# Moving ScalarE's slot for other stages' pieces from the head of a scan round to behind the first decay

## Chip, cores and metric

The kernel runs on one core of a Trainium2 chip. The metric is the device time of one execution in microseconds (us). An execution that the hardware profiler recorded gives the views shown here; times of the kernel before are given as a median of three further runs.

## What is computed

A network of four layers is applied to a tensor x of 4 images, 56 by 56 positions, 96 channels. Layer 0 and layer 1 are vision blocks whose heart is a selective scan over the 3136 positions of an image in four directions, for 192 channels with 16 states each. Layers 2 and 3 are an attention without softmax and a feed-forward network in rounded arithmetic. The part that takes nearly all the time is this recurrence, cut from the reference:

```python
dt = softplus(dt_raw @ dtw + dtb)
d_a = exp(dt[..., None] * a)                 # decay, per channel and state
d_b = dt[..., None] * b_ssm[:, :, None, :]
def step(h, inp):
    da_t, db_t, x_t, c_t = inp
    h = da_t * h + db_t * x_t[..., None]     # 192 x 16 states
    y_t = jnp.einsum('bds,bs->bd', h, c_t)
    return (h, y_t)
```

What stands around it are layer norms, projections, a convolution, SiLU, GELU and ReLU, all of them on the same 4 images.

## The kernel before

**The scan in rounds.** `scans` walks through 2 layers, 4 images, 4 directions and 7 chunks of 448 positions. A chunk has 8 rounds (two halves `e` of the channels, four quarters `q` of the states), so there are 1792 rounds. A round holds three groups `g` of 128 partitions by 448 positions. Round n consists of:

- `products(n)`: VectorE multiplies `du` with `b` for groups 0 and 1 into `h` (line 719). `b` is a row of matmul output on TensorE, made by `begin` a round ahead (`spread_b`, line 616, one PSUM buffer). The third group's product is made on GpSimd in `begin` (line 714).
- `scan(n, g)`, g = 0, 1, 2: VectorE runs the recurrence over the group (line 726) with the decay factors `da[g]` in PSUM.
- `decay(n + 1, g)`: ScalarE writes the next round's factors exp(na * dt) into `da[g]` (line 678). There is one `da` tile per group, so the decay of a group must wait for the scan of the same group in this round, and the next round's scan must wait for it.
- `kept(n)` and `carried(n + 2)`: ScalarE copies three columns that link one chunk to the next (lines 696 and 691); `h` has three buffers.
- `hc`: GpSimd multiplies the scanned states with `c` (line 767); two rounds later `add_up` has TensorE sum them into `y` (lines 794 and 798), and `keep_sums` has ScalarE copy `y` out every fourth round (line 805), between the second and the third decay.

**The chain to the next chunk's dt.** While a chunk is scanned, the next ones are prepared. `prepare` issues DMAs and a GpSimd multiplication (line 521); `prepare_on_scalar` has ScalarE do the copies to `cf` (lines 489, 491, 587) and the softplus (lines 506 and 508) in fixed rounds; `on_tensor` has TensorE do the matmuls of that chain (lines 448, 609, 496). The fetches of `cb`, `dt` and `du` are DMAs issued by SyncE.

**Pieces of other stages.** All other work (load, middle, branch, fuse, attend) is written as generators, cut into pieces at `yield`. A piece is run in one of two slots of a round: "F" pieces end in ScalarE work, "C" pieces are mostly TensorE and VectorE. `scans` yields "F" or "C" where a slot lies, and `overlap` then issues the pieces that are due and for which there is room: `spend` adds a piece's estimated ScalarE and TensorE time to a backlog, `half_round`, called twice a round, drains it by 0.9 and 2.4, and `room` admits a piece if the backlog with it stays within 4.0 and 7.0. A piece holds at most two PSUM banks (`ps`). Large F pieces contain a SiLU or GELU and hence two table loads (lines 903, 1065, 1074, 1102, 1115, with the return load of line 829), or two ReLU groups (lines 1260 to 1262). `keep_busy` puts warming matmuls with zeros (line 785) into TensorE's queue ahead of `begin`'s matmul, as many as the other work of the round leaves room for.

**Order.** The order on TensorE, ScalarE, VectorE and GpSimd is the order in which the Python code issues the instructions; each engine executes its own list in that order, and semaphores hold an instruction until its inputs and its buffer are there. SyncE's DMAs are placed by the framework's scheduler. So where `scans` yields a slot decides where on each engine's list the pieces stand.

Of the kernel before, what the change touches and what calls it, by code (L numbers as in the profile page):

```python
# [167 lines left out]
class Net:  # L168
# [454 lines left out]
    def scans(self):  # L623

        nc, sp = self.nc, self.sp
        chunks = []
        for l in range(2):
            for i in range(NB):
                for n, (orient, rev) in enumerate(ORDER[l]):
                    for step in range(NCS):
                        ch = Step()
                        ch.l, ch.i, ch.orient, ch.rev, ch.step = l, i, orient, rev, step
                        ch.k = 2 * orient + rev if l == 0 else orient + 2 * rev
                        ch.c = NCS - 1 - step if rev else step  # L640
                        ch.n, ch.first = n, n == 0 and step == 0
                        ch.skip = n == 0
                        ch.opening = ch.skip and (l, i) == (0, 0)
                        ch.last = n == 3 and step == NCS - 1
                        ch.cb, ch.dt, ch.du = [], [], []
                        chunks.append(ch)
        rounds = [(ch, e, q) for ch in chunks for e in range(NE) for q in range(NQ)]
        per = NE * NQ


        da = [self.psum.tile([128, 512], F32, name=f"da{g}")[:, : CS + 4] for g in range(NG)]
        for t in da:
            nc.vector.memset(t, 0.0)

        def steps(n):

            return [(ch, n - per * j) for j, ch in enumerate(chunks[max(0, n // per) : n // per + 3], max(0, n // per))]

        def ahead(n):
            for ch, o in steps(n):  # L660
                self.on_tensor(ch, o)

        for n in range(-14, 0):
            for ch, o in steps(n):
                self.prepare(ch, o)
            if n > -8:
                yield "F", n, 0
            for ch, o in steps(n):
                self.prepare_on_scalar(ch, o)
            ahead(n)  # L670
            if n > -8:
                yield "C", n, 0

        def decay(n, g):

            if n < len(rounds):
                ch, e, q = rounds[n]
                nc.scalar.activation(da[g][:, INNER], ch.dt[e][:, g], AF.Exp, scale=ch.par.na[:, e, q, g : g + 1])  # L678

        def column(t, at):  # L680

            return t[:, at : at + 2 * ROW + 1 : ROW]

        def carried(n):

            if n < len(rounds):
                ch, e, q = rounds[n]
                hs[n] = sp.tile([128, WIDE], F32, name="h", bufs=3)
                if not ch.step:
                    return  # L690
                nc.scalar.copy(column(hs[n], ROW if ch.rev else 1), ch.par.carry[:, e, q])  # L691

        def kept(n):
            ch, e, q = rounds[n]
            if ch.step < NCS - 1:
                nc.scalar.copy(ch.par.carry[:, e, q], column(hs[n], 2 if ch.rev else CS + 1))  # L696

        def own(n):
            ch, e, q = rounds[n]
            return NQ * e + q in (OWN_TAIL if ch.l and ch.i else OWN)  # L700

        hs, bs = {}, {}

        def tokens(t):

            return self.groups(t, 2)[:, :, :CS]

        def begin(n):

            if n < len(rounds):  # L710
                ch, e, q = rounds[n]
                bs[n] = self.spread_b(ch, q)
                if not own(n):
                    nc.gpsimd.tensor_tensor(tokens(hs[n])[:, 2], ch.du[e][:, 2], ch.cb[q][:, 1], ALU.mult)  # L714

        def products(n):
            ch, e, q = rounds[n]
            for g in range(3 if own(n) else 2):
                nc.vector.tensor_tensor(tokens(hs[n])[:, g], ch.du[e][:, g], bs[n], ALU.mult)  # L719

        def scan(n, g):
            ch, e, q = rounds[n]
            c = 1 if ch.step else 0
            way = slice(CS + 1 + c, 1, -1) if ch.rev else slice(2 - c, CS + 2)
            h = hs[n][:, g * ROW :]
            nc.vector.tensor_tensor_scan(h[:, way], da[g][:, way], h[:, way], 0.0, ALU.mult, ALU.add)  # L726

        carried(0)
        carried(1)
        begin(0)  # L730
        self.exp_and_ln()
        self.tables = True
        for g in range(NG):
            decay(0, g)
        late = []
        for n, (ch, e, q) in enumerate(rounds):
            r = NQ * e + q
            products(n)
            for c, o in steps(n):
                self.prepare(c, o)  # L740
            self.half_round()
            strided = [1.5 + 1.5 * ch.orient] * (r % NQ == 2)
            strided += [1.5 + 1.5 * c.orient for c, o in steps(n) for _ in self.projected(c, o)]
            self.spend((0.6, 0.7, 1.7, 0, 0, 0, 0.7, 0.6)[r], (1.3, 1.3, 0, 0, 0, 0, 0.4, 0.4)[r] + sum(strided))
            yield "F", n, r
            for c, o in steps(n):
                self.prepare_on_scalar(c, o)
            ended = late.pop(0) if len(late) == 2 else None
            if ended:
                self.keep_busy(ended[2])  # L750
            begin(n + 1)
            if ended:
                self.add_up(*ended)
            ahead(n)
            self.half_round()
            for g in range(NG):
                if g == 2 and ended and ended[2] == NQ - 1:
                    self.spend(0.6, 0)
                    self.keep_sums(*ended[:3])
                scan(n, g)  # L760
                if g == 2:
                    kept(n)
                decay(n + 1, g)
            yield "C", n, r
            carried(n + 2)
            hc = sp.tile([128, NG, CS], F32, name="hc", bufs=3)
            nc.gpsimd.tensor_tensor(  # L767
                hc, tokens(hs[n]), ch.cb[q][:, 0].unsqueeze(1).to_broadcast([128, NG, CS]), ALU.mult,
            )
            late.append((ch, e, q, hc))  # L770
            del hs[n], bs[n]
        for ended in late:
            self.add_up(*ended)
        self.keep_sums(ch, e, q)
        yield "C", len(rounds), 0
# [655 lines left out]
```

## Time and profile before

| | |
|---|---|
| median of three runs | 7943.03 us (7932.21 to 7953.92) |
| the profiled execution | 7941.06 us, span 7939.3 us |
| granted TensorE clock | 0.913 of full speed |
| rounds of the scan | 1792, between about 88 and 7725 us of the span |
| VectorE in that stretch | 7436 us busy of 7637 |
| ScalarE in that stretch | 5942 us busy |
| TensorE, GpSimd in that stretch | 6728 and 7132 us busy |

In the profile, DVE is VectorE, ACT ScalarE, PE TensorE, POOL GpSimd and SP SyncE. A row of the costliest groups gives line, engine, operation, output and inputs, shapes and count, then the busy time and the mean duration in ns, and after the second bar the time that the engine sat idle just before these instructions, with what ended most of that idling. A row of the waits gives who waited for whom, the total in us, the number of waits and the longest. A row of the timeline gives start and duration in us; "x3" stands for three merged neighbours.

### The profile page before, as it was taken

How to read it: one execution, taken by the hardware profiler on the slowest of the kernel's cores; microseconds unless marked ns; L12 is line 12 of the kernel's file. 1: busy time of each engine (PE TensorE's matmuls, PEld its weight loads, DVE VectorE, ACT ScalarE, POOL GpSimd, SP SyncE). 2: the span in 40 equal slices, each digit the busy share in tenths (PEclk: the TensorE clock that was granted, in tenths of full speed). 3: DMA queues.
4: the chain of work that ended last, by engine and by line, in shares of the span. 5: the costliest groups of instructions: out<-in, count | busy, mean ns of one | idle time of the engine just before them, and what ended most of it. 6: DMA issues, size and time to landing. Idle time of an engine off the chain costs nothing.

```text
span 7939.3 us, 113478 instructions
## 1 busy us (share of the span) xinstructions
PE 6970.5 (88%) x33762; PEld 2314.2 (29%) x33762; DVE 7516.4 (95%) x9603; ACT 6104.3 (77%) x12756; POOL 7165.1 (90%) x3989
## 2 busy tenths in 40 slices
PE   7888888889888988899889988998889988899888
PEld 3222223222222223222222222322233222322234
DVE  6999999999999999999999999999999999999983
ACT  6778878777787768887678876787877877778776
POOL 5999999999998999999999999999999999999981
PEclk8989989989999989989889899999999898998988
DMA  5555655567555765566655666555565555655551
GB/s 181 183 188 190 192 194 188 177 192 228 189 188 177 221 204 177 181 190 212 200 180 177 199 208 209 189 164 170 182 208 182 166 173 191 201 175 166 180 171 55
DMA packets 568240, 1467.54 MB, mean 185 GB/s; under 512 B 108034, under 2 KB 337156, under 8 KB 566756
## 3 DMA queue, kind: packets, MB, share of 16 engines
q1 hardware_dynamic: 566848, 1458.49, 57.7%
q8 instruction: 265, 4.34, 0.2%
q14 instruction: 355, 2.91, 0.1%
q10 hardware_dynamic: 772, 1.80, 0.1%
HBM read 1186.49 MB, written 273.47 MB: 184 GB/s over the span
## 4 chain that ended last, share of the span: by engine, by line
DVE 30%; PE 29%; ACT 19%; issue 14%; POOL 4%; DMA 3%; DVEq 0%; SPq 0%; POOLq 0%; ACTq 0%
DVE h L726 22%; DVE h L719 6%; ACT da L678 6%; PE y L798 6%; PE y L785 5%; PE y L794 3%; POOL hc L767 2%; PE b L616 2%; ACT L829 2%; PE ps L946 2%; ACT Y L805 1%; PE pp L496 1%; PE pp L448 1%; PE ps L823 1%; POOL h L714 1%
## 5 line engine op out<-in xcount | busy, mean ns | idle before, releaser
L726 DVE TENSOR_TENSOR_SCAN h<-da,h 128x449 f32<-128x449 f32 (+1 forms) x5376 | 5469.0, 1070 | 92.7 <-ACT da L678 76.1
L767 POOL TENSOR_TENSOR hc<-h,cb 128x1344 f32<-128x1344 f32 x1792 | 4883.8, 2725 | 456.7 <-DVE h L726 355.8
L678 ACT ACTIVATE da<-dt,na 128x448 f32<-128x448 f32 x5376 | 3342.9, 632 | 890.7 <-DVE h L726 875.7
L719 DVE TENSOR_TENSOR h<-du,b 128x448 f32<-128x448 f32 x3584 | 2023.4, 605 | 107.0 <-PE b L616 76.9
L798 PE MATMUL y<-hc,four 128*32 128x448 f32 x14336 | 1894.4, 603 | 12.3 <-POOL hc L767 12.0
L714 POOL TENSOR_TENSOR h<-du,cb 128x448 f32<-128x448 f32 x1792 | 1753.7, 979 | 45.2 <-ACT h L691 26.4
L785 PE MATMUL y<-w,zeros 128*96 128x448 bf16 x5140 | 1421.0, 395 | 0.0
L616 PE MATMUL b<-cf,sel 128*128 128x448 bf16 x1792 | 671.5, 375 | 605.1 <-DVE h L719 596.1
L785 PEld LDWEIGHTS <-zeros 128*96 128x96 bf16 x5140 | 632.5, 134 | 1172.1 <-issue 1011.5
L448 PE MATMUL pp<-U,wd 96*128 96x448 f32 x896 | 663.7, 829 | 10.0 <-DMA U<-u 4.2
L798 PEld LDWEIGHTS y<-hc,four 128*32 128x32 f32 x14336 | 293.8, 112 | 1134.4 <-issue 636.8
L794 PE MATMUL y<-Y,ident 96*96 96x448 f32 x672 | 538.0, 890 | 39.1 <-ACT Y L805 22.3
L496 PE MATMUL pp<-cf,wd 12*96 12x448 f32 (+1 forms) x896 | 464.5, 599 | 92.5 <-ACT dtc L506 51.2
L521 POOL TENSOR_TENSOR duc<-dtc,U 96x896 f32<-96x896 f32 x224 | 482.8, 2155 | 29.7 <-ACT dtc L508 29.7
L696 ACT COPY carry<-h 128x3 f32<-128x3 f32 x1536 | 301.8, 196 | 241.8 <-DVE h L726 232.6
L805 ACT COPY Y<-y 96x448 f32<-96x448 f32 x448 | 341.9, 763 | 28.6 <-PE y L798 27.9
L691 ACT COPY h<-carry 128x3 f32<-128x3 f32 x1536 | 280.9, 183 | 52.7 <-POOL hc L767 48.8
L587 ACT COPY cf<-pp 64x448 f32<-64x448 f32 x448 | 235.6, 526 | 86.8 <-PE pp L609 78.9
L506 ACT ACTIVATE dtc<-pp,wd 96x448 f32<-96x448 f32 x448 | 281.4, 628 | 15.5 <-PE pp L496 11.7
L616 PEld LDWEIGHTS <-sel 128*128 128x128 bf16 x1792 | 178.5, 100 | 373.1 <-issue 302.5
L823 PE MATMUL ps<-w,cen 96*96 96x448 f32 x458 | 232.7, 600 | 34.4 <-DVE w L1240 11.7
L496 PEld LDWEIGHTS pp<-cf,wd 12*96 12x96 f32 (+1 forms) x896 | 111.4, 162 | 452.9 <-ACT dtc L506 167.2
(383 smaller groups left out, 5354.5 us busy)
## 6 DMA issues: line engine op xcount, KB each, us to landing
cb<-cd SPq DMA_DIRECT2D x896, 448.0 KB, 4.9
dt<-dd SPq DMA_DIRECT2D x448, 672.0 KB, 5.6
du<-dd SPq DMA_DIRECT2D x448, 672.0 KB, 5.4
dd<-dtc SPq DMA_DIRECT2D x672, 112.0 KB, 2.0
dd<-duc SPq DMA_DIRECT2D x672, 112.0 KB, 2.0
win<-m SPq DMA_DIRECT2D x252, 112.0 KB, 4.8
U<-u SPq DMA_DIRECT2D x112, 168.0 KB, 4.6
w<-z SPq DMA_DIRECT2D x84, 224.0 KB, 4.2
```

The costliest lines, as they stand in the source:

```text
L448: self.nc.tensor.matmul(ch.ps.rearrange("p (a b) -> p a b", b=HS), ch.par.wx[:, e], self.in_order(self.U[e], ch.orient, ch.c * CS, CS), st ...
L496: self.nc.tensor.matmul(ch.pd, ch.par.wt[rows, C * e : C * e + C], ch.cf[rows], start=True, stop=True)
L521: self.nc.gpsimd.tensor_tensor(in_rows(ch.duc), in_rows(ch.dtc), u[:, :, lo : lo + CS // HS], ALU.mult)
L616: self.nc.tensor.matmul(ps, self.sel[:, q], self.upper(ch.cf), start=True, stop=True)
L678: nc.scalar.activation(da[g][:, INNER], ch.dt[e][:, g], AF.Exp, scale=ch.par.na[:, e, q, g : g + 1])
L714: nc.gpsimd.tensor_tensor(tokens(hs[n])[:, 2], ch.du[e][:, 2], ch.cb[q][:, 1], ALU.mult)
L719: nc.vector.tensor_tensor(tokens(hs[n])[:, g], ch.du[e][:, g], bs[n], ALU.mult)
L726: nc.vector.tensor_tensor_scan(h[:, way], da[g][:, way], h[:, way], 0.0, ALU.mult, ALU.add)
L767: nc.gpsimd.tensor_tensor(hc, tokens(hs[n]), ch.cb[q][:, 0].unsqueeze(1).to_broadcast([128, NG, CS]), ALU.mult,)
L785: self.nc.tensor.matmul(self.y[:C], self.zeros[:, :C], self.some, start=False, stop=False)
L794: nc.tensor.matmul(o, w, self.in_order(a, ch.orient, ch.c * CS, CS), start=True, stop=False)
L798: nc.tensor.matmul(self.y[32 * n : 32 * n + 32], self.four, hc[:, g], start=n == 3, stop=n == 3 or q == NQ - 1,)
```

## The change

Before, a round yields the F slot at its head: ahead of `prepare_on_scalar`, of `begin(n + 1)`, of the scans and of the first decay. After, it yields F inside the loop over the groups, behind `scan(n, 0)` and `decay(n + 1, 0)`, ahead of `scan(n, 1)`. On ScalarE's list the pieces thus move past `prepare_on_scalar` and the first decay; they now stand between the first and the second decay. On TensorE's list F pieces have next to nothing; on GpSimd's, the few multiplications that F pieces hold move past the product of line 714. As F now comes behind the second `half_round`, the backlog has been drained twice and not once when F pieces ask for room; C pieces find the same draining as before. The DMAs that F pieces issue keep their place between those of `prepare` and of `keep_sums` in the written order.

```diff
@@ -742,7 +742,6 @@
             strided = [1.5 + 1.5 * ch.orient] * (r % NQ == 2)
             strided += [1.5 + 1.5 * c.orient for c, o in steps(n) for _ in self.projected(c, o)]
             self.spend((0.6, 0.7, 1.7, 0, 0, 0, 0.7, 0.6)[r], (1.3, 1.3, 0, 0, 0, 0, 0.4, 0.4)[r] + sum(strided))
-            yield "F", n, r
             for c, o in steps(n):
                 self.prepare_on_scalar(c, o)
             ended = late.pop(0) if len(late) == 2 else None
@@ -761,6 +760,8 @@
                 if g == 2:
                     kept(n)
                 decay(n + 1, g)
+                if g == 0:
+                    yield "F", n, r
             yield "C", n, r
             carried(n + 2)
             hc = sp.tile([128, NG, CS], F32, name="hc", bufs=3)
```

Line numbers in this document are those of the kernel before; in the kernel after, lines 746 to 763 have a number lower by one, and those from 764 on a number higher by one.

## The prediction

> **What bounds the kernel now.** I read the page first: busy shares, then the costliest groups.
>
> ```profile
> span 7939.3 us, 113478 instructions
> PE 6970.5 (88%) x33762; PEld 2314.2 (29%) x33762; DVE 7516.4 (95%) x9603; ACT 6104.3 (77%) x12756; POOL 7165.1 (90%) x3989
> ...
> L726 DVE TENSOR_TENSOR_SCAN h<-da,h 128x449 f32<-128x449 f32 (+1 forms) x5376 | 5469.0, 1070 | 92.7 <-ACT da L678 76.1
> ...
> L678 ACT ACTIVATE da<-dt,na 128x448 f32<-128x448 f32 x5376 | 3342.9, 632 | 890.7 <-DVE h L726 875.7
> L719 DVE TENSOR_TENSOR h<-du,b 128x448 f32<-128x448 f32 x3584 | 2023.4, 605 | 107.0 <-PE b L616 76.9
> ```
>
> VectorE is 95% busy, and two lines make it: three scans (L726) and two products (L719) in each of 1792 rounds. Their starts in the timeline put an undisturbed round at about 4.0 us: 1.12 for the products, about 1.0 from scan to scan. What VectorE waits for is the third column: 92.7 us before scans, mostly for the decay factors `da` from ScalarE, and 107.0 before products, mostly for `b` from TensorE. So only about 200 us can be won in the scan part; there is no such ceiling on what can be lost. Next, whom VectorE waits for:
>
> ```profile
> DVE h L719 <- PE b L616: 76.9, 87, 9.6
> DVE h L726 <- ACT da L678: 76.1, 158, 1.9
> ```
>
> The 76.1 us fall on 158 waits. To see which, I took one round with a large foreign piece from the timeline, ScalarE and then VectorE (start, duration, engine):
>
> ```profile
> 3258.70 0.18 ACT L691 COPY h<-carry 128x3 f32<-128x3 f32 x1
> 3258.89 1.28 ACT L1074 ACT_TABLE_LOAD   x1
> 3260.19 1.16 ACT L1074 ACTIVATE w<-ps,b 128x448 f32<-128x448 f32 x2
> 3261.36 1.28 ACT L829 ACT_TABLE_LOAD   x1
> 3262.66 1.20 ACT L678 ACTIVATE da<-dt,na 128x448 f32<-128x448 f32 x2
> ```
>
> ```profile
> 3258.96 3.05 DVE L726 TENSOR_TENSOR_SCAN h<-da,h 128x449 f32<-128x449 f32 x3
> 3261.93 1.12 DVE L719 TENSOR_TENSOR h<-du,b 128x448 f32<-128x448 f32 x2
> 3263.33 2.07 DVE L726 TENSOR_TENSOR_SCAN h<-da,h 128x449 f32<-128x449 f32 x2 [0.28 <-ACT da L678]
> ```
>
> The first scan ends at 3260.03 (start plus 1.07); call it 0. ScalarE is free from -1.15, but the next decay can't start before 0, as it overwrites the `da` that this scan reads. The piece uses that gap: it runs from -1.14 to +2.61, the decay follows, and VectorE, ready at +3.02 (end of the products), waits 0.28 us. The head of the round is where a large piece costs least.
>
> **What the Trainium skill says.** "ScalarE: Activation LUTs", section "What ACT_TABLE_LOAD costs", gives about 1283 ns for a table load and a further drain of about 1380 ns. The trace agrees with the first (1283 ns) and shows no drain: the ACTIVATE starts 1.30 us after the load. I use the trace. "Perfetto Trace Analysis", section "Identifying the Most-Contended Engine", has the engine with the highest occupancy as the one to look at; that is VectorE here, and its waits explain the time. "Advanced Engine Details and Errata", section "Sequencer Loop", has engine instructions wait in a queue for their semaphores; the trace agrees as far as it goes: ScalarE runs its listed order, with every decay behind the piece listed before it.
>
> **The change part by part.** Nothing is computed more or less. In the instruction order of both programs, 837 rounds have foreign ScalarE work ahead of the first decay before (1356 us by the trace's durations); after, 46 with 26 us still do (pieces begun in the other slot), and 847 with 1338 us have it between first and second decay. Large blocks, over 2.7 us, are as many: 209 before, 206 after. So the earlier draining of the backlog hardly changes the packing: 0, at most 10 us either way.
>
> *First decay.* It no longer waits for a piece. Over all rounds with pieces I added up the waits of the first scan on its decay: 67 us, 48 of them behind large blocks and 19 behind small ones whose TensorE input was late. All go: **-67**.
>
> *Second decay.* In the round above the first decay runs from +0.04 to +0.67, the block takes 3.77 (3258.89 to 3262.66) to +4.44, the second decay ends at +5.07, and VectorE sees it at about +5.11. VectorE, no longer held at the first scan, wants the second at +4.02 (products +3.02, one scan step 1.00). It waits 1.09. In general the wait is block minus 2.68 us, so any piece under 2.7 is free; of the 837 rounds some 630 are, covered by a slack of about 2.2 us that decays have in rounds without a piece. The large blocks, from the table-load rows: L903 56 and L1074 28 at 3.77 (84 x 1.09 = 92 us); L1115 28 at 3.51 (28 x 0.83 = 23); L1065 and L1102 56 at 3.24 (56 x 0.56 = 31); and some 40 double ReLU blocks (L1260 to L1262, twice) at 3.58 (40 x 0.90 = 36). Sum 182.
>
> *Third decay.* In some 50 of these rounds the copy L805 (0.5 to 1.0 us) and the carry copy L696 (0.2) stand between second and third decay; the third is then late by another half microsecond: 25. Where VectorE has one more operation in the round (0.6 us, as L888) or came late anyway, the waits shrink; I take off 17. New waits on decays: **+190** (170 to 230).
>
> *The chain to dt (L489, L587, L506, L508).* It stays at the head and is no longer behind a piece. At 2493.87 a piece with table loads (L1102) held L506 until 2497.11; TensorE's L496 sat idle 2.02 us for it, 6.75 us of convolution stood behind that, `b` came late, and VectorE lost 4.54 us, the largest such wait of this kind in that stretch. Products waiting for `b` two rounds after a large block make about 30 us in 27 rounds (all such gaps, tallied from the trace, 90 us in 120 rounds). Part comes back, since the convolution also needs a bank that the piece itself frees, now later: **-20** (0 to -30).
>
> *TensorE behind the pieces.* A piece ends later by about 1.9 us. TensorE's matmuls of the same round that read its result, or reuse its bank, wait with it, and the next `b` is queued behind them. In the written order some 70 rounds have this dependence on a block of 2.5 us or more. The trace of before can't show it, as it has those pieces early; VectorE is itself 1 us late in these rounds, which covers most. Bound: 0 to 70; I take **+10**. The 125 more warming matmuls (L785, 5140 before, 395 ns) are 49 us of a queue with 12% idle: 0; without that cover some tens of us.
>
> *Queues passed.* On SyncE the stores behind a piece (L912, L922, L1111, L1120) wait up to 1.9 us longer for ScalarE and hold the fetches of `cb`, `dt` and `du` behind them; those are issued three rounds, 12 us, ahead and land in 5 to 6: 0, with some us of cover left. On GpSimd only the 27 multiplications of L931 pass the product L714; L1285 and L1213 wait longer for ScalarE, and hold hc (L767): 0, bound 20. ScalarE's wait for a free `h` (L691) has about 2 us in hand.
>
> Sum: -67 + 190 - 20 + 10 = **+113 us** against the profiled execution of 7941.06 (span 7939.3): 8054. The median shown, 7943.03, is 2 us higher, inside its own spread of 7932 to 7954.
>
> **The rivals.**
> *TensorE gets late too* (0.15). For: in-order queue, 88% busy, PSUM banks shared. Against: VectorE's new lateness covers it. 113 + 60 = 173: 8114 and up.
> *The head of the chain is what counts, and it is faster* (0.05). With the chain to dt always first, TensorE is never held and `b` never late: up to 107 us at L719 and the 67 at L726 come back, 174 in all. That decides only if the new waits on the second decay come to less than that: if they were half of my sum (95), 7862. Against it: 4.54 us is a rare case, only a third of these gaps follows large blocks, and the block and its window are measured.
> *It balances* (0.05). New waits fall in rounds where VectorE would have waited for `b` anyway, and the lateness is shared: within 24 us of 7941.
> *The change does nothing* is excluded by the order: the pieces move in nearly all of 837 rounds.
>
> **How the numbers follow.** My forecast, second decay late, has 0.75 and runs from 7991 (new waits 170, and half of L719's 107 back: 7941 - 67 + 170 - 53) to 8094 (new waits 230: 7941 - 67 + 230 - 20 + 10). With part of the first rival the range is 7990 to 8130. A measurement of this kernel can tell about 0.3%, 24 us, from no change. Slower by more: 0.75 + 0.15 = 0.90; within: 0.05; faster: 0.05.
>
> **What would show it.** In the profile after: the wait of L726 on L678 at 180 to 250 us instead of 76, in some 200 waits near 0.5 to 1.2, at the second scan and not the first; VectorE's busy time unchanged; ScalarE's idle time before L678 up; L719's wait on `b` below 77. I am wrong if L726's wait falls, or if L719's wait on `b` is what grows (first rival).

## The result and the profile after

The kernel after takes 8083.4 us (median of four runs, 8079.6 to 8087.3), the kernel before in the same runs 7938.7. The ratio is 1.0177 (95% interval 1.0165 to 1.0189): slower by about 142 us. The profiled execution after has a span of 8081.2 us against 7939.3, 141.9 more. The times of before differ a little from one set of runs to the next (medians 7939 to 7953), so the experiments are compared by their ratios to before.

These are the rows of the page after that answer to those shown before: the span, the busy shares, scans, decays and products.

```profile
span 8081.2 us, 113950 instructions
PE 7074.1 (88%) x33887; PEld 2349.2 (29%) x33887; DVE 7528.8 (93%) x9603; ACT 6079.6 (75%) x12756; POOL 7169.9 (89%) x3989
...
L726 DVE TENSOR_TENSOR_SCAN h<-da,h 128x449 f32<-128x449 f32 (+1 forms) x5376 | 5491.8, 1069 | 212.8 <-ACT da L678 192.7
...
L678 ACT ACTIVATE da<-dt,na 128x448 f32<-128x448 f32 x5376 | 3377.0, 632 | 1316.8 <-DVE h L726 1295.4
L719 DVE TENSOR_TENSOR h<-du,b 128x448 f32<-128x448 f32 x3584 | 2021.5, 604 | 117.8 <-PE b L616 68.8
```

VectorE has the same 9603 instructions. Its idle time before scans went from 92.7 to 212.8 us (+120), before products from 107.0 to 117.8 (+11), and the scans' own busy time from 5469.0 to 5491.8 (+23). That is more than the whole loss; other groups give a little back. ScalarE sits idle before decays for 1317 us instead of 891: it now waits for the first scan's end with a piece in hand that it could have run.

A round with the same piece (GELU twice, line 1075 after, 1074 before), ScalarE and then VectorE:

```profile
3348.25 0.64 ACT L678 ACTIVATE da<-dt,na 128x448 f32<-128x448 f32 x1 [1.19 <-DVE h L726]
3348.91 1.28 ACT L1075 ACT_TABLE_LOAD   x1
3350.20 1.16 ACT L1075 ACTIVATE w<-ps,b 128x448 f32<-128x448 f32 x2
3351.38 1.28 ACT L830 ACT_TABLE_LOAD   x1
3352.68 0.64 ACT L678 ACTIVATE da<-dt,na 128x448 f32<-128x448 f32 x1
```

```profile
3347.14 3.04 DVE L726 TENSOR_TENSOR_SCAN h<-da,h 128x449 f32<-128x449 f32 x3
3350.11 1.12 DVE L719 TENSOR_TENSOR h<-du,b 128x448 f32<-128x448 f32 x2
3351.15 1.08 DVE L726 TENSOR_TENSOR_SCAN h<-da,h 128x449 f32<-128x449 f32 x1
3353.35 2.08 DVE L726 TENSOR_TENSOR_SCAN h<-da,h 128x449 f32<-128x449 f32 x2 [1.11 <-ACT da L678]
```

The bracket in ScalarE's first row is the 1.19 us that it stood idle. The piece runs from 3348.91 to 3352.66, and the second decay follows. The second scan could have started at about 3352.15, 1.00 us after the first; it starts at 3353.35, 1.20 us later. The profile shows 1.11 us of this as idle time, since it counts from the end of the first scan's record, and undisturbed scans overlap a little in the records. Before, the same piece cost 0.28 us of idle time at the first scan.

By scan, tallied over all rounds from the trace: before, 77 us of decay waits, nearly all at the first scan; after, none at the first, 179 at the second (196 times) and 18 at the third (48 times). Such tallies are also made below for the waits for `b`. They give larger sums for `b` than the profile's row of L719 waiting for L616, which puts some of these waits down to other instructions: the tally has 92 us before and 104 after, the row 76.9 and 68.8. The idle time before products as a whole (107.0 and 117.8 us) moves as the tally does.

### The profile page after: what moved, and what is told of

Same layout as the page of the kernel before. It is cut to its first block, busy times and chain, and to the rows that moved or that the text cites. A ratio compares the mean times of both kernels' runs of the same rounds, so it can differ in the third digit from the quotient of the medians.

```text
span 8081.2 us, 113950 instructions
## 1 busy us (share of the span) xinstructions
PE 7074.1 (88%) x33887; PEld 2349.2 (29%) x33887; DVE 7528.8 (93%) x9603; ACT 6079.6 (75%) x12756; POOL 7169.9 (89%) x3989
## 5 line engine op out<-in xcount | busy, mean ns | idle before, releaser
L726 DVE TENSOR_TENSOR_SCAN h<-da,h 128x449 f32<-128x449 f32 (+1 forms) x5376 | 5491.8, 1069 | 212.8 <-ACT da L678 192.7
L678 ACT ACTIVATE da<-dt,na 128x448 f32<-128x448 f32 x5376 | 3377.0, 632 | 1316.8 <-DVE h L726 1295.4
L719 DVE TENSOR_TENSOR h<-du,b 128x448 f32<-128x448 f32 x3584 | 2021.5, 604 | 117.8 <-PE b L616 68.8
L786 PE MATMUL y<-w,zeros 128*96 128x448 bf16 x5265 | 1460.8, 397 | 0.0
L616 PE MATMUL b<-cf,sel 128*128 128x448 bf16 x1792 | 677.8, 378 | 496.8 <-DVE h L719 489.6
L786 PEld LDWEIGHTS <-zeros 128*96 128x96 bf16 x5265 | 653.1, 134 | 1197.8 <-issue 1034.6
L795 PE MATMUL y<-Y,ident 96*96 96x448 f32 x672 | 544.6, 900 | 75.5 <-ACT carry L696 43.0
L496 PE MATMUL pp<-cf,wd 12*96 12x448 f32 (+1 forms) x896 | 468.8, 604 | 34.4 <-ACT dtc L506 17.9
L691 ACT COPY h<-carry 128x3 f32<-128x3 f32 x1536 | 281.1, 183 | 49.1 <-POOL hc L768 46.6
L616 PEld LDWEIGHTS <-sel 128*128 128x128 bf16 x1792 | 178.9, 100 | 376.1 <-issue 303.5
L863 PE MATMUL ps<-rsb,ident 128*96 128x112 f32 x1784 | 236.3, 280 | 29.4 <-ACT rsb L858 22.6
```

What stands on the lines that cost most here:

```text
L496: self.nc.tensor.matmul(ch.pd, ch.par.wt[rows, C * e : C * e + C], ch.cf[rows], start=True, stop=True)
L616: self.nc.tensor.matmul(ps, self.sel[:, q], self.upper(ch.cf), start=True, stop=True)
L786: self.nc.tensor.matmul(self.y[:C], self.zeros[:, :C], self.some, start=False, stop=False)
L795: nc.tensor.matmul(o, w, self.in_order(a, ch.orient, ch.c * CS, CS), start=True, stop=False)
```

## Experiments

The theory: the loss is the second decay, late behind large blocks. The rivals: TensorE is late behind the pieces; the chain to dt or the packing of pieces matters more than the place of the decay.

### The chain first, the slot still at the head

```diff
-            yield "F", n, r
             for c, o in steps(n):
                 self.prepare_on_scalar(c, o)
+            yield "F", n, r
             ended = late.pop(0) if len(late) == 2 else None
```

> The slot stays at the head of the round, but behind the copies and softplus of the chain to dt and ahead of begin and of the first decay: the half of the change that puts the chain first, without the half that puts the first decay first. Theory (the loss is the second decay waiting behind large blocks, and the chain is a small gain): all of the chain and of the block still stand ahead of the first decay, so decay waits stay near 77 us; the waits for b that come from L496 waiting for ScalarE (32 us of 92 in the trace of before, 1 us after) go. About 7915, from 7900 to 7930; L726's wait on L678 70 to 85 us, none at the second scan. Rival (the new order of the chain, or TensorE, is what loses): slower than before, 8000 or more.

Measured: ratio 0.9944 (0.9931 to 0.9956), 7897.7 us. So putting the chain first is by itself a gain of about 45 us. The row of L496 on TensorE, before and in this kernel (after the last bar: idle time before it, and who ended most of it):

```profile
L496 PE MATMUL pp<-cf,wd 12*96 12x448 f32 (+1 forms) x896 | 464.5, 599 | 92.5 <-ACT dtc L506 51.2
```

```profile
L496 PE MATMUL pp<-cf,wd 12*96 12x448 f32 (+1 forms) x896 | 460.7, 595 | 25.9 <-ACT dtc L506 13.7
```

TensorE's idling there falls from 92.5 to 25.9 us, and VectorE's waits for `b`, in my tally, from 92 to 67. Decay waits are 70 us, none at the second scan. The time is just below the range that was expected, and the waits moved as expected.

### The slot just before the first scan

```diff
             self.half_round()
+            yield "F", n, r
             for g in range(NG):
```

(with the chain first, as above.)

> The slot lies behind begin, the sums and the second draining of the backlog, and just ahead of the first scan and first decay. Against the kernel after it differs by one thing in ScalarE's list: the first decay stands behind the piece. The room that the backlog gives is that of the kernel after. Theory: like the first experiment, 7915 (7900 to 7930), so all of the loss lies in the one exchange of piece and first decay. Rival (the draining twice before F packs pieces badly): about 8080, as after, or at least half of the loss, over 8005.

Measured: ratio 0.9987 (0.9979 to 0.9995), 7932.8 us. Against the kernel after, which differs from it in ScalarE's list by the exchange of piece and first decay alone, it is 0.0190 of the time faster: about 151 us. VectorE's wait on decays, here and in the kernel after:

```profile
DVE h L726 <- ACT da L678: 89.1, 135, 2.0
```

```profile
DVE h L726 <- ACT da L678: 192.7, 233, 1.5
```

So the loss is that exchange. But the kernel is 34 us slower than the first experiment, and missed its range: decay waits are 89 us instead of 70, and `b` waits 75 instead of 67. In the written order large blocks fall in rounds with chain work of over 0.4 us 102 times instead of 61, and block and chain together exceed 4.2 us in 39 rounds instead of 4. TensorE's list also has the 125 more warming matmuls. So draining twice before F pieces ask for room costs something, by packing or by these matmuls; the two stand together here.

### Large and small pieces in different slots

```diff
-                if place[0] == self.slot and held ...
+                mine = {"L": "F" if act > 2.7 else "", "S": "F" if act <= 2.7 else ""}.get(self.slot, self.slot)
+                if place[0] == mine and held ...
```

`scans` yields "L" at the head, behind the chain, and "S" behind the first decay; in the next experiment the letters change places.

> Two slots: F pieces with an estimate over 2.7 us at the head (behind the chain), all others behind the first decay. Theory: only large blocks overrun the window at the second decay; small ones are free there and no longer hold the first decay when their input is late (19 us of waits in before). About 7900 (7880 to 7920); decay waits 50 to 65 us, all at the first scan behind large blocks. Rival (any piece behind the first decay costs, since its results reach TensorE later): 7960 or more, with waits on b above 92 us.

Measured: ratio 0.9936 (0.9924 to 0.9949), 7896.9 us. Decay waits 66 us, 64 of them at the first scan; `b` waits 61. Some 630 small pieces behind the first decay cost nothing. They also bring nothing that can be told from the first experiment.

> The opposite division: pieces up to 2.7 us at the head (behind the chain), large ones behind the first decay. Theory: it keeps the whole loss, since some 206 large blocks stand before the second decay: 8085 to 8105, decay waits at the second scan 170 to 190 us as after, and 10 to 20 us at the first scan. Rival (small pieces cause a good part of the loss): 8030 or less.

Measured: ratio 1.0152 (1.0139 to 1.0166), 8063.5 us: nearly the whole loss with only the some 206 large blocks behind the first decay.

```profile
DVE h L726 <- ACT da L678: 199.6, 238, 1.8
```

By scan, decay waits are 186 us at the second, 12 at the third and 5 at the first. The total is 20 us below the range that was expected; why is open, as the division changes the packing as well.

### The slot behind the second and the third decay

```diff
-                if g == 0:
+                if g == 1:        # and in the other kernel: g == 2
                     yield "F", n, r
```

> The slot lies behind the second decay instead of the first. Theory (a block must fit between the moment its slot opens and the moment the next decay is wanted; a decay can't start before its scan ends, and the window is the same one scan later): the third decay is late by block minus about 2.55 us, since the carry copy now stands between as well; decay waits 200 to 240 us, all at the third scan, 8080 to 8110. Rival (the harm is particular to the second decay, or shrinks the later the slot lies): 8040 or less.

Measured: ratio 1.0340 (1.0324 to 1.0355). Decay waits are 260 us at the third scan, somewhat over what was expected, but the time is 110 us over the top of the range. VectorE's idle time against before grew by 187 us ahead of scans, by 39 ahead of products and by 37 ahead of all its other work. The first of these is the third scan's waits less those that went at the first scan, about as expected; the expectation had nothing for the other two.

> The slot lies behind the third decay. There ScalarE has no decay to do until the first scan of the next round ends, about 1.15 us later, so the block uses that gap as at the head of the round; the chain and the carry copy into h (L691) stand behind it. Theory: decay waits back at 70 to 95 us, at the first scan, and the chain late as in before: 7940 to 7970, a little over before because GpSimd's product (L714) waits for the carry copy. Rival (any slot inside the loop costs as much as the one behind the first decay): 8040 or more.

Measured: ratio 1.0609 (1.0593 to 1.0625), the slowest of all; the expectation was wrong by some 470 us. VectorE's and then TensorE's waits in this kernel:

```profile
DVE h L719 <- PE b L616: 274.2, 249, 10.0
DVE w L1082 <- PE ps L1080: 61.5, 25, 3.6
DVE h L719 <- ACT h L691: 56.2, 74, 2.6
DVE w L1192 <- ACT w L1190: 48.0, 28, 7.8
```

```profile
PE b L616 <- DVE h L719: 342.1, 344, 2.2
PE ps L863 <- ACT rsb L858: 125.0, 107, 3.2
PE ps L1280 <- ACT hq L1263: 77.7, 72, 2.2
PE ps L852 <- ACT w L838: 59.8, 68, 2.2
```

The decays are in order, as expected: hardly any wait on them is left (18 us in my tally). But the C slot follows at once. TensorE's matmuls of that slot (L863, L1280, L852) need what the F pieces of the same round have yet to compute; TensorE waits for ScalarE, the next `b` stands behind those matmuls, and VectorE waits 274 us for `b` instead of 77. The carry copy L691, which also stands behind the piece now, holds products for another 56 us (3 before). The expectation looked at ScalarE's list, and beyond it only at GpSimd's product. The traces of before, after and these two show one row: `b` waits in my tally of 92, 104, 133 and 342 us as the slot moves back. This agrees with the reading that the later F lies, the less time ScalarE has before the C slot asks for its results; no run moved the C slot to test it.

### After, with the sums copied first

```diff
-                if g == 2 and ended and ended[2] == NQ - 1: ...
                 if g == 0:
+                    if ended and ended[2] == NQ - 1:
+                        self.spend(0.6, 0)
+                        self.keep_sums(*ended[:3])
                     yield "F", n, r
```

> The kernel after, with one more move: every fourth round the copy of the sums (L805) stands ahead of the piece and not between the piece and the third decay. Theory of what is left over the decay waits (TensorE's first matmul of the next sums, L794, waits for this copy behind the block, and then b is late): waits on b fall from 104 to 75 to 90 us, the third decay's from 18 to under 8, the second decay's stay at 170 to 185: 8045 to 8065. Rival (b is late because TensorE waits for the results of the pieces themselves): waits on b stay near 104, 8070 or more.

Measured: ratio 1.0144 (1.0128 to 1.0159), 0.33 points under after, some 26 us. Both kernels' first two rows of VectorE's waits, after and then this one:

```profile
DVE h L726 <- ACT da L678: 192.7, 233, 1.5
DVE h L719 <- PE b L616: 68.8, 89, 9.6
```

```profile
DVE h L726 <- ACT da L678: 240.4, 245, 3.2
DVE h L719 <- PE b L616: 45.1, 63, 9.7
```

TensorE's row of the next sums' first matmul (L794 before, L795 in the other two), before, after and here:

```profile
L794 PE MATMUL y<-Y,ident 96*96 96x448 f32 x672 | 538.0, 890 | 39.1 <-ACT Y L805 22.3
```

```profile
L795 PE MATMUL y<-Y,ident 96*96 96x448 f32 x672 | 544.6, 900 | 75.5 <-ACT carry L696 43.0
```

```profile
L795 PE MATMUL y<-Y,ident 96*96 96x448 f32 x672 | 535.4, 886 | 0.0
```

Waits for `b` fall more than expected (in my tally from 104 to 56), and none that follows a wait of L795 is left, where after had about 30 us. So that copy, stuck behind a block, is the main path that these traces show by which the piece's new place makes `b` late. The move isn't quite alone: its `spend` moves with it, so there are 5086 warming matmuls instead of 5265, and in the order of ScalarE's list large blocks meet chain work in 84 rounds instead of 102. The third decay's waits vanish. But ScalarE now waits for the sums ahead of the block (174 us instead of 30), and the second decay's waits rise to 240 us, where 170 to 185 were expected. The net came out at the upper end of what was forecast, by larger terms of both signs.

### After, with the old room for pieces

```diff
             ahead(n)
-            self.half_round()
             for g in range(NG):
...
                 if g == 0:
                     yield "F", n, r
+                    self.half_round()
```

> The kernel after, with the second draining of the backlog moved behind the slot, so that F pieces find the room they had in before. In the written order this puts large blocks in rounds with chain work 61 times instead of 102. Theory with packing as a term of its own (the second experiment was some 35 us slower than the first, with that packing as their main difference): 8045 to 8065, with the decay waits at 175 to 195 us. Rival (behind the first decay the chain lies in the gap of 1.15 us ahead of that decay, so it doesn't matter which round a block meets): 8075 to 8090, as after.

Measured: ratio 1.0141 (1.0124 to 1.0158), about 29 us under after by the ratios; by the profiled executions 15 (span 8065.7). The decay waits are the same 190 us, and `b` waits 108 against 104. So some 15 to 30 us of the loss come from the earlier draining, by packing or by the 125 warming matmuls that go with it; the trace's waits don't show where, and I leave that open.

### Without table loads

```diff
-            nc.scalar.activation(g[0], ps[0], AF.Gelu, bias=self.b1[:, :1])
+            nc.scalar.activation(g[0], ps[0], AF.Identity, bias=self.b1[:, :1])
...
     def exp_and_ln(self):
+        if self.tables:
+            return
```

(every SiLU and GELU likewise, in the kernel before and in the kernel after; so these two kernels compute something else, and leave out the loads.)

> The kernel before with SiLU and GELU replaced by the identity with the same bias, and the loads of activation tables in the scan part left out (that part of the computation is changed); estimates, and so the order, stay. Blocks of 3.2 to 3.8 us shrink to 0.6 to 1.3; only some 40 double ReLU blocks stay large. Theory: of the 77 us of decay waits at the first scan about 25 to 35 stay; the chain is held less, b waits fall by some 20: 7860 to 7890. It is the base for the next run.

> The same part of the computation changed in the kernel after. Theory (only blocks over about 2.7 us cost behind the first decay): the waits of the second decay fall from 179 to 30 to 45 us (40 ReLU blocks at 0.75 to 1), and the distance between the kernels shrinks from 145 us to 10 to 45. Rival (what costs is the number of pieces in the new place, their order among the other queues, or the packing): a distance of 90 us or more stays.

Measured: 0.9882 (0.9867 to 0.9897) for before, 0.9917 (0.9903 to 0.9930) for after; 7855.4 and 7881.5 us. The distance shrinks from 142 to 26 us by the medians (9.5 by the two profiled executions). VectorE's wait on decays, before and after, without table loads:

```profile
DVE h L726 <- ACT da L678: 37.2, 55, 1.5
```

```profile
DVE h L726 <- ACT da L678: 39.2, 58, 1.5
```

The pieces are as many, in the same places and the same order; only their length is less. The second decay's waits fall from 179 to 33 us, about what the 40 ReLU blocks give. This is the size of the block as a cause, shown by taking it away. The decay waits of the two kernels are now equal, so the 26 us have another cause, which is open.

### Looking for the better kernel

The first and third experiments each with the copy of the sums behind the first decay:

```diff
-                if g == 2 and ended and ended[2] == NQ - 1:
+                if g == 1 and ended and ended[2] == NQ - 1:
```

> The first experiment's kernel (slot at the head, chain ahead of it), and the copy of the sums moved from between second and third decay to between first and second. Theory: in the first experiment 21 of 67 us of b waits came from L794 waiting for that copy; most of these go, and the second decay, which has 0.5 us and more in hand, pays little, though ScalarE may now wait for the sums themselves: 15 to 25 us faster than the first experiment, ratio to before 0.991 to 0.993. Rival (ScalarE's wait for the sums makes the second decay late): no faster than the first experiment, 0.9944 or more.

> The third experiment's kernel (large pieces at the head, small ones behind the first decay) with the same early copy of the sums, which then stands ahead of the small pieces' end and behind the first decay. Theory: b waits from 61 to about 45 us, decay waits 65 to 80: ratio to before 0.991 to 0.9935. Rival (small pieces and the copy together overrun the second decay): 0.995 or more, with over 40 us of waits at the second scan.

Measured: 0.9924 (0.9911 to 0.9937) and 0.9922 (0.9910 to 0.9935). Waits for `b` fall to 48 and 47 us in my tally; the second scan waits 12 and 20 us for its decay. Both beat before by 0.8%, about 60 us. Neither can be told from the other, nor for certain from the first experiment (0.9944), whose interval overlaps theirs; what the early copy adds in time isn't shown, though `b` waits are fewer. Of the two, the one with a single slot at the head is the simpler.

## Why the prediction was right

It said slower, by the second decay behind large blocks, 8054 us with a range of 7990 to 8130; 8083 was measured. The loss is 142 us where the sum gave 113. By its steps:

- **First decay, -67:** right. Its waits went from 77 us to nothing.
- **Second and third decay, +190:** 197. The wait of 1.09 us, worked out from the window of 2.68, is 0.02 less than the idle time in the round shown; the waits at the second scan came 196 times for 206 blocks. From start to start the delay there is 1.20: the prediction put VectorE's wish for the second scan at the end of the first one's record, and an undisturbed scan starts 0.08 us before that. The removal of the table loads (33 us left at the second scan) and the division of large and small pieces (186 us from the large ones alone) show that nearly all of these waits come from the size of the block.
- **The chain to dt, -20:** the mechanism was right, the size too small. Waits for `b` two rounds after a large block went from 31 us to 3, and the first experiment shows the chain alone to be worth about 45 us of time.
- **TensorE behind the pieces, +10 (0 to 70):** mis-sized. The other waits for `b` rose by about 40 us (from 61 to 101 in my tally), so that those in total rose by 12 and did not fall. The sign that was named, L719's wait on `b` below 77, came in the profile's row (68.8), but not in the tally nor in the idle time before products. The prediction priced the matmuls that read a piece's result; it named the copy L805 only for the third decay. The copy also frees the bank for the next sums, L794 waits for it, and the next product row `b` waits behind L794. With the sums copied first, L795 no longer waits at all and the waits for `b` are 56 us.
- **Packing, 0 to 10:** too small. The earlier draining, which moved large blocks into rounds with chain work and added the warming matmuls, costs 15 to 34 us in the two pairs that show it. I had counted how many blocks there were, and not which rounds they fell in.
- **Not in the sum:** scans that follow each other overlap by about 0.08 us in the records (start to start 1.00, duration 1.07 to 1.08), and a wait between two scans breaks such a joint. Of 3584 joints 3553 overlap before and 3283 after; 270 at 0.08 us are about 21 of the 23 us by which the scans' busy time grew. First scans, which no longer wait, give back about 12 us by the same overlap with the product ahead of them: VectorE's whole busy time grew by 12.

The main mechanism, the second decay behind large blocks, was right and so was its size. That the whole sum came within 29 us is in part luck: the gain from the chain and the loss behind the sums were both taken too small, and they are of opposite sign.

From kernel to kernel: the chain first is -0.56%; the slot behind the sums, with its other packing, +0.43%; the exchange with the first decay +1.90%. That is the 1.77% of the change. The first rival (TensorE late) is real as a mechanism but small in this kernel; it becomes the larger cost when the slot moves on to behind the third decay. The second (the chain decides and it is faster) had the right sign for a half of the change, but 45 us came of it and not up to 174, and the other half costs three times as much.

One rival was not named and has no run of its own: the granted TensorE clock is 0.899 in the profiled execution after and 0.913 before. Over all recorded runs of the kernel before, the times tend to be longer at a lower clock (7963 us at 0.907, 7939 at 0.915). But the kernel with the sums copied first has 0.900, and its products wait for `b` 56 us where before has 92, so the lower clock alone doesn't make `b` late; and the waits on decays, which are most of the loss, come after ScalarE's work. What the clock adds beyond these waits isn't separated.

## What to carry to other kernels

Where an engine executes its list in order, price a moved block by its window: from the moment its new place opens to the moment the next instruction behind it is wanted, less that instruction's own time; what fits costs nothing, and what doesn't is lost on nearly every occurrence (196 of 206 here). A place ahead of an instruction that must wait anyway gives the block that wait for free. Then look at the other end: who reads the block's result or waits for its buffer in the same round, and what is queued behind that reader; and where a planner gives room by a backlog, look at which rounds large pieces fall in, not only at how many there are.

## What was not expected of the hardware

Back-to-back scans of 128 by 449 overlap by about 0.08 us in the records (1.07 to 1.08 us each, 1.00 apart), so a wait between two costs that much more than the idle time that it shows. An activation table load took 1.28 us, and the instruction behind it started 1.30 us after the load's start (the median, in every kernel here). No further drain was seen: in the round shown, two loads and two ACTIVATEs took 3.75 us together.
